# Column sums of a symmetric softmax for two more groups: sixteen accumulating transfers replaced by GpSimd additions

## The chip, the cores and the metric

The kernel runs on one core of one Trainium2 chip. The metric is the device time of one execution in microseconds (us). TensorE is called PE below, VectorE DVE, ScalarE ACT, GpSimd POOL, and the engine whose queue issues most transfers SP, as in the profile.

## The reference, cut to what matters

Four images of 64 x 64 positions with 64 channels, all float32, pass through four layers. Layer 0 is a self-attention over the 4,096 positions of an image, layer 1 a convolution block with a 3 x 3 depthwise convolution, layer 2 an attention without weights, layer 3 a non-local block. The change lies in layer 2, which reads:

```
xf = x.reshape(B, C, N)                        # C = 64, N = 4096, of the array as it lies
scores = einsum('bci,bcj->bij', xf, xf)        # symmetric
attn = softmax(scores, axis=-1)
out = einsum('bcj,bij->bci', xf, attn) + x
```

Layer 1, which the kernel interleaves with it, contains `y = y1 * y2`, `w = mean(y) @ sca_w + sca_b`, `y = y * w`, `y @ pw2_w`: the mean over all positions must be there before the product with `pw2_w`.

## The kernel before, in words

**Layer 2.** The 4,096 rows and columns of the score matrix are split into 8 groups of 512. An item `n` of `layer2` makes one block of 128 x 1024 exponentials: four products on PE (`score`, L1391, with `X` in the tile `ko`), then two exponentials on ACT (L1396), each followed by the read of its row-sum accumulator. The scores are symmetric, so a block of group h can also serve as the mirrored block of group g. For such a mirrored block DVE transposes the exponentials in 32 x 32 pieces (`turned`, L1409), PE multiplies them later (`turned_products`, L1479), and its row sums in the mirror are the column sums of the block: `column_sums` (L1413 to L1434) adds all mirrored blocks of a group into a tile `esum`, folds it once (L1434, 128 x 512) and `spread_sums` (L1442, L1443, DVE) reduces it, nine items after the group's last mirrored block in image 0. Not mirrored blocks are multiplied by `products` (L1453), two or three items behind their score. At a group's end the accumulated products are copied by ACT (L1462 and L1465, tile `own`) and added by DVE into the result `A` (L1468).

**Image 0 and the others.** Images 1 to 3 have a fixed list of groups (`FULL`); POOL adds the column sums there (L1432). Image 0 has the list `PART`: groups 0, 1, 2, 3, 4, 7, 6, 5 in this order, of which groups 0, 1, 6 and 5 have mirrored blocks: 8, 4, 8 and 8. For group 0, POOL adds. For groups 1, 6 and 5 (`moved`), POOL only issues transfers: the first two write the two halves of `esum`, each later one is an accumulating transfer into one half, and a last one adds the halves (L1426, L1430). Two transfers into the same half must follow one another, so POOL waits for the landing of the last but one before it issues the next.

**What sets the order.** The instruction order of PE, ACT, DVE and POOL is written out by hand. Image 0's layer 2 has lanes beside it, generators that advance by estimated times: in the stretch of groups 6 and 5 the lane `conv` runs layer 1 of image 3, and the lane `misc` runs `features2` of image 1 (L1303 to L1314, tile `ko`). In this stretch DVE has, in its order: the last taps of image 3's depthwise convolution (L1241), two multiplications with accumulated sums (L1252: `yg<-y,yg`), their reduction to `ytot` (L1258), the addition of group 7's `own` into `A` (L1468), the four transposes of group 6's first mirrored blocks, then `ch` (L1263, from PE's product L1261 of `ytot`) and `pw2s` (L1265). PE's product L1270 needs `pw2s`.

**Buffers.** Exponentials live in pairs of blocks in tiles of 128 x 2048 from a pool `ep` of six (`new_e`), which `own`, `esum` and image 0's weights tile `xr` (L1361) share. A block's tile is free when its products, its transpose and its column-sum operation (transfer or addition) have read it. In the built program, the ACT block of item 78 (the first not mirrored block after group 6's first four mirrored ones) takes over the tile that was group 7's `own`, and so waits for the DVE addition L1468.

## Time and profile before

| | us |
|---|---|
| median of three runs (2452.43 to 2452.67) | 2452.49 |
| the profiled execution: its time | 2456.51 |
| the profiled execution: its span, first to last instruction | 2454.7 |
| busy PE, of the span | 2417.0 (98%) |
| busy DVE / ACT / POOL | 1479.3 / 1644.3 / 540.9 |
| POOL additions L1432, 128 x 1024: 154 | 2.37 each |
| column-sum transfers L1426: 20, of 512 KB (and 3 by L1430) | 5.5 from issue to landing (median, L1426) |

The profile is one execution, 4.0 us longer than the median of the timed runs and with 1.8 us outside its span. The stretch of the change is the last part of image 0's layer 2: group 6's mirrored blocks stand at 1175 to 1205 us of the span, group 5's at 1214 to 1254.

How to read the lines shown later. A line of the timeline has the start in the span, the time, engine, source line, operation, output<-inputs, shapes, a count, and in brackets the idle time before it with what ended it. Starts overlap with the end of the instruction before[...]. A line of the windows has the stretch, its length, and busy time (and count) of PE, of PE's weight loads, DVE, ACT and POOL, then PE's clock, the busy share of the DMA engines and GB/s. POOL's busy time doesn't count the issue of transfers.

### The profile page before, as it was taken

Reading aid. Unit: us, or ns where it says so; the run is one execution under the profiler, and the core shown is the slowest. Engines: PE = TensorE matmul, PEld = TensorE weight load, DVE = VectorE, ACT = ScalarE, POOL = GpSimd, SP = SyncE. Lnnn points to the kernel's source line nnn. Section 1 sums busy time; section 2 is a strip of 40 time slices with the busy share of each in tenths; the row PEclk is TensorE's granted clock in tenths of the full one; section 3 lists DMA queues with packets and bytes.
Section 4 is the critical chain, followed back from the end, with each engine's and each line's share of the span. In section 5 each row is a group of like instructions: output and inputs, shape, how many; then the busy total and the mean of one; then the engine's idle time right before and its main releaser. Section 6 shows DMA issues by size and latency. Waiting matters only on the chain.

```text
span 2454.7 us, 63654 instructions
## 1 busy us (share of the span) xinstructions
PE 2417.0 (98%) x27509; PEld 916.3 (37%) x27509; DVE 1479.3 (60%) x1794; ACT 1644.3 (67%) x3140; POOL 540.9 (22%) x381
## 2 busy tenths in 40 slices
PE   9999999999999999999999999999999999999998
PEld 3343453336333633343334442144431344421113
DVE  2020278227832773378656668876668866678886
ACT  4656766676666676668654459954479744579996
POOL 2000000000000000120135561255631365622110
PEclk9999999999999999999999999999999999999999
DMA  3000000000000000120630027610075300286554
GB/s 80 1 18 1 19 1 18 18 19 1 18 18 16 4 19 18 35 63 2 136 72 20 19 67 134 139 27 23 16 150 119 78 20 20 71 168 142 120 118 117
DMA packets 66373, 131.68 MB, mean 54 GB/s; under 512 B 12860, under 2 KB 34085, under 8 KB 66085
## 3 DMA queue, kind: packets, MB, share of 16 engines
q0 software_dynamic: 23024, 81.83, 16.5%
q1 hardware_dynamic: 42309, 43.85, 7.9%
q8 instruction: 218, 3.57, 0.6%
q10 hardware_dynamic: 752, 1.85, 0.2%
q14 instruction: 70, 0.57, 0.1%
HBM read 4.80 MB, written 4.19 MB: 4 GB/s over the span
## 4 chain that ended last, share of the span: by engine, by line
PE 86%; DVE 8%; ACT 4%; issue 1%; SPq 0%; DMA 0%; DVEq 0%; ACTq 0%
PE PS L1096 18%; PE PS L1122 18%; PE PS L1391 10%; PE PS L1453 10%; PE PS L1646 8%; PE PS L1707 8%; PE PS L1479 7%; DVE tg L1698 3%; PE PS L1206 2%; ACT e L1657 2%; ACT e L1396 1%; DVE X L1568 1%; PE PS L1561 1%; PE PS L1064 1%; PE PS L1171 1%
## 5 line engine op out<-in xcount | busy, mean ns | idle before, releaser
L1101 ACT ACTIVATE e<-PS 128x1024 f32<-128x1024 f32 x512 | 524.2, 1024 | 339.4 <-PE PS L1096 306.3
L1396 ACT ACTIVATE e<-PS 128x512 f32<-128x512 f32 x632 | 371.6, 596 | 342.0 <-PE PS L1391 321.1
L1096 PE MATMUL PS<-X,q 64*64 64x512 f32 x4096 | 573.9, 591 | 2.3 <-DVE X L979 1.7
L1122 PE MATMUL PS<-e,vq 64*64 64x512 f32 x4096 | 575.3, 592 | 0.0
L1657 ACT ACTIVATE e<-PS 128x512 f32<-128x512 f32 (+2 forms) x588 | 500.2, 921 | 59.0 <-PE PS L1646 38.1
L1698 DVE TENSOR_TENSOR tg<-tg,e 128x2048 f32<-128x2048 f32 x172 | 393.8, 2290 | 42.8 <-ACT e L1657 30.9
L1391 PE MATMUL PS<-ko 64*64 64x512 f32 x2528 | 335.6, 596 | 2.6 <-DVE u L1291 1.5
L1453 PE MATMUL PS<-e,X 64*64 64x512 f32 x2528 | 329.9, 590 | 2.5 <-issue 1.4
L1432 POOL TENSOR_TENSOR esum<-esum,e 128x1024 f32<-128x1024 f32 x132 | 314.0, 2379 | 59.7 <-ACT e L1396 52.4
L1241 DVE SCALAR_TENSOR_TENSOR y<-pad,vec,y 128x1024 f32<-128x1024 f32 x240 | 308.8, 1287 | 18.2 <-ACT y L1237 10.9
L1432 POOL TENSOR_TENSOR esum<-e 128x1024 f32<-128x1024 f32 x22 | 52.2, 2373 | 1206.2 <-ACT e L1396 1187.3
L1409 DVE STREAM_TRANSPOSE turned<-e 128x1024 f32<-128x1024 f32 x196 | 240.6, 1238 | 106.0 <-ACT e L1396 105.8
L1646 PE MATMUL PS<-tg,ph 32*64 32x512 f32 x4096 | 295.1, 612 | 1.7 <-ACT e L1657 0.8
L1096 PEld LDWEIGHTS PS<-X,q 64*64 64x64 f32 x4096 | 183.0, 133 | 261.8 <-issue 181.6
L1122 PEld LDWEIGHTS PS<-e,vq 64*64 64x64 f32 x4096 | 183.1, 133 | 253.8 <-issue 158.1
L1707 PE MATMUL PS<-e,tg 128*32 128x512 f32 x2048 | 272.5, 604 | 0.0
L1109 DVE TENSOR_REDUCE sums<-zs 128x1 f32<-128x4 f32 x128 | 19.6, 153 | 276.4 <-ACT e L1101 276.2
L1679 POOL DMA_DIRECT2D xn<-e x116 | 101.0, 892 | 292.3 <-ACT e L1657 206.0
L1453 PEld LDWEIGHTS PS<-e,X 64*64 64x64 f32 x2528 | 98.0, 133 | 176.3 <-issue 156.7
L1391 PEld LDWEIGHTS PS<-ko 64*64 64x64 f32 x2528 | 90.5, 132 | 169.9 <-issue 145.7
L1646 PEld LDWEIGHTS PS<-tg,ph 32*64 32x64 f32 x4096 | 63.4, 129 | 222.9 <-ACT e L1657 190.5
L1396 ACT ACTIVATION_READ_ACCUMULATOR e<-PS 128x1 f32 x632 | 127.3, 201 | 0.0
(219 smaller groups left out, 1692.4 us busy)
## 6 DMA issues: line engine op xcount, KB each, us to landing
xn<-e POOLq DMA_DIRECT2D x132, 512.0 KB, 5.4
esum<-e POOLq DMA_DIRECT2D x20, 512.0 KB, 5.5
xn<-t SPq DMA_DIRECT2D x64, 128.0 KB
ph<-tg SPq DMA_DIRECT2D x64, 128.0 KB
xn<-X SPq DMA_DIRECT2D x224, 32.0 KB
xr<-X SPq DMA_DIRECT2D x176, 32.0 KB
ko<-ko SPq DMA_DIRECT2D x32, 128.0 KB
xr<-in_x_dram SPq DMA_DIRECT2D x13, 256.0 KB
```

The source lines that it names most:

```text
L1096: mm(ps[64 * c : 64 * c + 64, bass.ts(r, 512)], m.q[rows_, 128 * t + 64 * c : 128 * t + 64 * c + 64], x[rows_, bass.ts(g, 512)], start=Tru ...
L1101: act(es[g // 2][:, bass.ts(g % 2, 1024)], ps, AF.Exp, bias=SHIFT0, accum_out=zs[:, g : g + 1],)
L1122: ins = mm(PS[64 * s : 64 * s + 64, 2048 + 512 * j : 2560 + 512 * j], vq[rows_, :], es[j // 2][rows_, k : k + 512], start=t == 0 and i < 2 ...
L1241: stt(y1, win, wt, y1, ALU.mult, ALU.add)
L1391: mm(ps[64 * c : 64 * c + 64, bass.ts(r, 512)], m.ko[rows_, k : k + 64], m.ko[rows_, bass.ts(h, 512)], start=True, stop=True,)
L1396: act(e[:, bass.ts(r, 512)], ps[:, bass.ts(r, 512)], AF.Exp, bias=SHIFT2, accum_out=slot(g, 2 * u + r),)
L1432: nc.gpsimd.tensor_add(esum, st["e"][mine_t[h][0]] if k == 1 else esum, e)
L1453: mm(st["acc"][r][64 * c : 64 * c + 64, :], xw[rows_, 4 * g + 2 * u + c, :], st["e"][n][rows_, bass.ts(c, 512)], start=n == mine[h][0], st ...
L1646: mm(PS[64 * c : 64 * c + 64, bass.ts(banks[k], 512)], m.ph[32 * k : 32 * k + 32, 128 * mc + 64 * c : 128 * mc + 64 * c + 64], m.th[32 * k ...
L1657: act(e[:, 512 * lo : 512 * k], PS[:, 512 * banks[lo] : 512 * banks[lo] + 512 * (k - lo)], AF.Exp,)
L1698: nc.vector.tensor_add(esum, esum, e)
L1707: mm(st["y"][32 * k : 32 * k + 32, :], m.gx[:, i % 32, :], es[i][:, bass.ts(k, 512)], start=mc == 0, stop=i % 32 == 31,)
```

## The change

In image 0, only group 1 keeps its transfers. Groups 6 and 5 are treated as group 0 and the other images are:

```
             k, e = mine_t[h].index(n), st["e"][n]
-            moved = b == 0 and h > 0
+            moved = b == 0 and h == 1
             if k == (0 if moved else 1):
                 st["esum"][h] = new_e("esum")
```

For each of the two groups, eight transfers L1426 and one L1430 go, and seven additions L1432 (128 x 1024) come. The fold L1434 stays. The tile `esum` is now taken at the second mirrored block instead of the first; no other tile of the pool is taken between the two. In the built program the instruction orders of PE, ACT and DVE are the same as before, and in POOL's order only these rows differ. What ACT and DVE wait for changes with it: where the reuse of a tile waited for a transfer's landing, it now waits for POOL's addition. POOL's first addition of group 6 waits for the second mirrored block's exponentials and for a DVE instruction that is long done.

More of the change, by code (lines that the diff above doesn't have):

```diff
@@ L1417, in column_sums @@
             k, e = mine_t[h].index(n), st["e"][n]
-            moved = b == 0 and h > 0
+            moved = b == 0 and h == 1
             if k == (0 if moved else 1):
```

## The prediction

> **What bounds the kernel now.** I read the page first: PE is busy 98% of the span, and the chain that ended last runs 86% through PE. So time is won or lost only where PE stands still, and each such place counts in full. The windows then say where that is, in the stretch of the change.

> ```profile
> PE 2417.0 (98%) x27509; PEld 916.3 (37%) x27509; DVE 1479.3 (60%) x1794; ACT 1644.3 (67%) x3140; POOL 540.9 (22%) x381
> ...
> PE 86%; DVE 8%; ACT 4%; issue 1%; SPq 0%; DMA 0%; DVEq 0%; ACTq 0%
> ```

> ```profile
> 1176.00:1204.00 28.00, 28.00 (x329) 9.95 (x321) 16.81 (x25) 17.54 (x52) 6.38 (x8) 1.00 0.83 180
> 1215.00:1241.00 26.00, 22.20 (x277) 9.24 (x278) 17.37 (x21) 13.53 (x40) 5.54 (x7) 1.00 0.92 200
> 1241.00:1260.00 19.00, 17.54 (x243) 6.93 (x239) 5.07 (x7) 10.76 (x31) 3.00 (x3) 1.00 0.47 90
> ```

> While group 6 is summed (first row) PE never idles: there is nothing to win there, and something to lose. While group 5 is summed it idles 3.8 us, and 1.5 us behind it. PE's waits in that time name five gaps: 0.83, 0.95 and 0.66 us behind `ko` copies (ACT waits for DVE's copy; no column sum is in that chain), and these two from its timeline:

> ```profile
> 1239.85 0.64 PE L1453 MATMUL PS<-e,X 64*64 64x512 f32 x2 [1.37 <-issue]
> ...
> 1257.51 1.08 PE L1391 MATMUL PS<-ko 64*64 64x512 f32 x6 [1.46 <-DVE u L1291]
> ```

> The first waits for nothing that the program names. It is the only such gap over 0.4 us in the kernel. The packets of PE's instruction queue (16 KB each) explain it: up to it PE began 515 instructions since the last fetch (1215.2, next 1237.4 us). The next longest such runs, 437 and 424, are in the same transfer-laden stretch, all others are at most 383. Fetches are late behind the transfers (DMA engines 92% busy). The second gap is DVE's lateness; its timeline beside POOL's shows why:

> ```profile
> 1253.77 1.76 DVE L1468 TENSOR_TENSOR A<-own,A 128x512 f32<-128x512 f32 x1 [4.21 <-ACT own L1465]
> ...
> 1253.72 1.26 POOL L1434 TENSOR_TENSOR esum<-esum 128x512 f32<-128x512 f32 x1 [3.76 <-DMA esum<-esum]
> ```

> L1468 takes 0.69 us alone (median of 14); here it ends 0.55 us after POOL's fold, 1.07 late.

> **The rule behind this.** [...] the 196 transposes L1409 take 1187 to 1247 ns, though most lie beside POOL additions, while L1298 (two SBUF inputs) takes 691 ns alone and up to 2435 beside one. [...]

> ```profile
> 1609.24 0.69 DVE L1736 SCALAR_TENSOR_TENSOR inv<-inv 128x512 f32<-128x512 f32 x1
> 1609.85 0.08 DVE L1736 DVE_READ_ACCUMULATOR inv<-inv 128x1 f32 x1
> 1609.97 2.73 DVE L1737 SCALAR_TENSOR_TENSOR yz<-inv,yz 128x512 f32<-128x512 f32 x1
> ...
> 1609.71 2.44 POOL L1432 TENSOR_TENSOR esum<-e 128x1024 f32<-128x1024 f32 x1 [26.84 <-ACT e L1396]
> ...
> 1612.22 2.71 POOL L1432 TENSOR_TENSOR esum<-esum,e 128x1024 f32<-128x1024 f32 x1
> ```

> POOL arrives during L1736, gets in 0.55 us after that one's start (2.44 instead of 2.36), DVE's next is held until POOL's end plus 0.55, and POOL's next addition is held 0.35. They alternate. The forecast goes by these durations.

> **The change part by part.**

> *POOL's work.* It loses 18 issues of about 0.86 us and their waits, and gains 14 x 2.37 = 33.2 us of additions. POOL isn't the bound: group 6's blocks come from 1176 to 1199 us, seven additions are 16.6 us, and no SP or ACT queue is passed. Tiles of exponentials come free earlier (addition ends instead of landings 5.5 us after issue); nothing on ACT's path waited for a landing, so this is worth 0.

> *Group 6: the new lock.* Here is DVE's order where the first addition now falls:

> ```profile
> 1177.19 0.69 DVE L1252 SCALAR_TENSOR_TENSOR yg<-y,yg 128x512 f32<-128x512 f32 x1
> 1177.81 0.08 DVE L1252 DVE_READ_ACCUMULATOR yg<-y,yg 128x1 f32 x1
> 1177.81 0.69 DVE L1252 SCALAR_TENSOR_TENSOR yg<-y,yg 128x512 f32<-128x512 f32 x1
> 1178.42 0.08 DVE L1252 DVE_READ_ACCUMULATOR yg<-y,yg 128x1 f32 x1
> 1178.54 0.16 DVE L1258 TENSOR_REDUCE ytot<-ysum 128x1 f32<-128x8 f32 x1
> 1178.62 0.68 DVE L1468 TENSOR_TENSOR A<-own,A 128x512 f32<-128x512 f32 x1
> ```

> ACT's last accumulator read for the second block starts at 1177.14; other additions start at the earliest 0.28 us after such a read's start, so POOL arrives at 1177.42, during the first L1252, and gets in at 1177.74. By the episode's steps:
> - addition 1: 1177.74 to 1180.10. The second L1252 ends at 1180.65 instead of 1178.50.
> - addition 2 (block ready at 1179.2): 1180.52 to 1182.88. L1258 needs no lock (1180.85, still ahead of PE's L1261 at 1181.30); L1468 ends at 1183.43 instead of 1179.30.
> - addition 3: 1183.30 to 1185.66. DVE's four transposes (4.54 us, no lock) run from 1183.36 and L1263 starts at 1187.90, L1265 (`pw2s`) at 1188.11.
> - ACT's item 78 waits for L1468: 1183.5 instead of 1181.42. Items 79 and 80 queue behind it; item 80's last read moves from 1186.39 to about 1186.95, so addition 4 is at 1187.2 to 1189.6. PE's L1391 for item 80 is held about 0.5 us by this, inside the stall below.
> - `pw2s` has one SBUF input, but 64, 128 and 256 columns of such an operation take 254, 287 and 341 ns: 0.45 ns a column against 1.3 for the whole 512-column L1468. [...] it is held: until 1189.7. No row shows one beside POOL; unheld it ends at 1188.4.

> PE's L1270, queued behind nothing at 1185.20, then starts at 1189.75: PE stands 4.55 us (3.2 if `pw2s` isn't held). All of PE, and ACT behind it, moves by this. Later collisions in group 6 (three of the four L1277, about 1.2 us each) end before their readers (ACT's L1165 had 1 to 3 us in hand): 0. **+4.55.**

> *Group 5: the relief.* The transfers' load goes (nine of 512 KB, 4.7 MB, between 1215 and 1254; SP's `xn` and `ko` transfers, 16 of 128 KB, stay), so the fetch is in time: **-1.37**. The fold L1434 follows the last addition at about 1241 instead of 1253.72, so L1468 at 1253.77 meets no lock and PE's 1.46 gap shrinks: **-1.07**. Now L1192 (twice, 1238.4, two SBUF inputs) meets the last addition and the fold: it ends at about 1243.1 instead of 1240.8, and PE needs it at 1247.6 at the earliest: 0. Other DVE work there is transposes and copies from PSUM; L1494's copies from PSUM show the same 414 ns beside POOL as alone: 0. The `ko` gaps stay.

> *Sum.* 4.55 - 1.37 - 1.07 = +2.1 us: the profiled 2456.5 would be 2458.6, and the median, 4.0 below its profile, **2454.6**. Against no change, this kernel's measurement tells about 0.2%, 4.9 us.

> **The rivals.**
> - *POOL comes second (ends faster).* If the two L1252, issued back to back with no wait, keep the pair, addition 1 starts at 1178.36, only L1468 is held (to 1181.27), `pw2s` ends at 1186.2 ahead of addition 4, and PE stands 1.05 us: -1.4, **2451.1**. It decides at 1177.81, 0.4 us after POOL's reckoned arrival. For it: these two have no semaphore between them, the episode's pair had. Against it: 0.07 us lie between the release (0.55 after start) and the second's start.
> - *`pw2s` isn't held:* 3.2 - 2.44 = +0.8, **2453.3**.
> - *The fetch stays late (ends slower).* The lock's stall comes, but SP's own `ko` transfers (1224 to 1240 us) are enough to hold PE's fetch back, so the 1.37 stays: 4.55 - 1.07 = +3.5, **2456.0**. It decides where a fetch run passes some 500 instructions. For it: the gap lies in the `ko` transfers' time. Against it: all three runs over 383 lie where the column sums' transfers do, two of them without `ko` transfers.
> - *The change doesn't do what it says:* excluded, POOL's rows are replaced in the built order and no other order moves.

> **How the numbers follow.** Forecast 0.50 (2454.6, own range 2453.5 to 2455.7), `pw2s` not held 0.12, POOL second 0.15, fetch stays late 0.15, something unlisted 0.08. The range leaves out little more than the last: from POOL second, 2451.1, less 0.3 for the steps' rounding, to 2457.4: the fetch and L1468's 1.07 both not won back (2457.0) and 0.4 for a longer hold. Slower by over 0.2% would need even more than that (2457.4): some of the last two cases, 0.11. Faster by over 0.2% would need all gaps of both groups gone and no stall: 0.02. Within: 0.87.

> **What would show it.** Right: L1252's second and L1468 near 2.8 and 2.7 us at 1178 to 1184; PE L1270 with 4 to 5 us idle before it, released by DVE `pw2s`; no gap without a named wait near 1242, and fetch runs under 400; the last L1468 pair, near 1256 us, back at 0.69 each. Wrong: L1270 without a gap; or a new wait of ACT for POOL behind a tile; or idle PE in group 5 as before.

## The result, and the profile after

| | median, us | runs | lowest to highest |
|---|---|---|---|
| before | 2452.49 | 11 | 2451.61 to 2453.84 |
| after | 2458.60 | 11 | 2457.47 to 2460.41 |

The ratio is 1.0025, 95% interval 1.0016 to 1.0034: the change costs 6.1 us, against a forecast of 2.1 us over the median. The profiled execution of after took 2458.60 us (span 2456.8) and stands at its own median. That of before (2456.51) stood 4.0 above, which turns out to matter. (The title's sixteen transfers are the L1426. Twelve of them accumulate, the first two of each group only write; two accumulating L1430 went with them.)

From the page of after, the busy line and the shares of the chain: PE is still busy 98% of the span, DVE's part of the chain has grown from 8% to 10%.

```profile
PE 2417.7 (98%) x27509; PEld 915.7 (37%) x27509; DVE 1489.3 (61%) x1794; ACT 1642.8 (67%) x3140; POOL 562.5 (23%) x377
...
PE 84%; DVE 10%; ACT 4%; issue 1%; SPq 1%; DMA 0%; DVEq 0%; ACTq 0%
```

The windows of after (stretch, length, PE, PEld, DVE, ACT, POOL, PE's clock, DMA share, GB/s):

```profile
1176.00:1204.00 28.00, 24.11 (x270) 7.95 (x262) 21.43 (x23) 12.29 (x37) 14.95 (x6) 0.94 0.16 39
1215.00:1241.00 26.00, 23.59 (x328) 10.40 (x316) 15.41 (x21) 14.15 (x39) 14.15 (x6) 1.00 0.40 81
1241.00:1260.00 19.00, 18.60 (x268) 7.64 (x260) 10.59 (x13) 11.24 (x33) 4.50 (x2) 1.00 0.01 3
```

In group 6 (first row) PE, which never idled, now idles 3.9 us, and its clock is 0.94 instead of 1.00. In group 5 the two gaps of the first profile of before are gone (PE 23.59 for 22.20, and 18.60 for 17.54). The timelines of DVE and of POOL in group 6:

```profile
1177.08 0.08 DVE L1252 DVE_READ_ACCUMULATOR yg<-y,yg 128x1 f32 x1
1177.08 2.84 DVE L1252 SCALAR_TENSOR_TENSOR yg<-y,yg 128x512 f32<-128x512 f32 x1
...
1180.03 2.64 DVE L1468 TENSOR_TENSOR A<-own,A 128x512 f32<-128x512 f32 x1
1182.60 4.61 DVE L1409 STREAM_TRANSPOSE turned<-e 128x1024 f32<-128x1024 f32 x4
1187.14 0.17 DVE L1263 TENSOR_SCALAR ch<-PS,vec 128x1 f32<-128x1 f32 x1
1187.34 1.66 DVE L1265 TENSOR_SCALAR pw2s<-pw,ch 128x64 f32<-128x64 f32 x1
```

```profile
1176.72 2.64 POOL L1432 TENSOR_TENSOR esum<-e 128x1024 f32<-128x1024 f32 x1 [83.05 <-ACT e L1396]
1179.44 5.46 POOL L1432 TENSOR_TENSOR esum<-esum,e 128x1024 f32<-128x1024 f32 x2
1186.62 2.34 POOL L1432 TENSOR_TENSOR esum<-esum,e 128x1024 f32<-128x1024 f32 x1 [1.71 <-ACT e L1396]
```

POOL's first addition slips in behind the first L1252, the second L1252 and L1468 are each held by one addition (2.84 and 2.64 us for 0.69), the transposes run at their usual rate beside POOL (four in 4.61 us, 4.62 before), and `pw2s` lies inside POOL's fourth addition: 1.66 us for 0.25. “The lock” stands here for just this holding of one engine's operation by the other's; in the prediction, the one that runs meanwhile has “the pair”. PE's timeline shows who waits for `pw2s`:

```profile
1183.51 1.66 PE L1391 MATMUL PS<-ko 64*64 64x512 f32 x8
1189.06 1.72 PE L1270 MATMUL PS<-yg,pw2s 128*64 128x512 f32 x4 [3.89 <-DVE pw2s L1265]
1190.71 1.99 PE L1453 MATMUL PS<-e,X 64*64 64x512 f32 x8
```

PE is idle 3.89 us, and 0.6 more is lost inside the row before (L1391 takes 1.66 for 1.04: item 80's second half waits). But look at the durations *behind* the gap: L1270 x4 takes 1.72 us and L1453 x8 takes 1.99, where the kernel before had no gap and these times:

```profile
1185.20 1.08 PE L1270 MATMUL PS<-yg,pw2s 128*64 128x512 f32 x4
1186.21 1.09 PE L1453 MATMUL PS<-e,X 64*64 64x512 f32 x8
```

The windows of two microseconds of after say why:

```profile
1186.00:1188.00 2.00, 0.00 (x0) 0.00 (x0) 1.97 (x4) 0.47 (x2) 1.39 (x1) 1.00 0.23 57
1188.00:1190.00 2.00, 0.94 (x4) 0.20 (x4) 2.00 (x2) 0.00 (x0) 0.95 (x1) 0.84 0.21 54
1190.00:1192.00 2.00, 2.00 (x10) 0.30 (x8) 0.52 (x2) 0.78 (x1) 0.00 (x0) 0.50 0.20 50
1192.00:1194.00 2.00, 2.00 (x52) 1.13 (x56) 0.33 (x1) 0.00 (x0) 0.00 (x0) 0.81 0.20 49
1194.00:1196.00 2.00, 2.00 (x88) 1.61 (x73) 0.00 (x0) 0.00 (x0) 0.00 (x0) 1.00 0.17 41
```

**Bookkeeping.** I compare the starts of the same PE instructions in two traces. Against a later, undisturbed profile of before (e1, 2452.46 us), after is 0.17 us late at the start of the stretch, 4.76 late at L1270 and 6.37 at 1225 us, where it stays. So the stall is 4.59, and the slow clock 1.61. Their sum, 6.2, is the whole measured difference of 6.1.

### The profile page after: what moved, and what is told of

Same layout as the page of the kernel before. It is cut to its first block, busy times and chain, and to the rows that moved or that the text cites. A ratio compares the mean times of both kernels' runs of the same rounds, so it can differ in the third digit from the quotient of the medians.

```text
span 2456.8 us, 63634 instructions
## 1 busy us (share of the span) xinstructions
PE 2417.7 (98%) x27509; PEld 915.7 (37%) x27509; DVE 1489.3 (61%) x1794; ACT 1642.8 (67%) x3140; POOL 562.5 (23%) x377
## 4 chain that ended last, share of the span: by engine, by line
PE 84%; DVE 10%; ACT 4%; issue 1%; SPq 1%; DMA 0%; DVEq 0%; ACTq 0%
PE PS L1096 18%; PE PS L1122 18%; PE PS L1453 8%; PE PS L1391 8%; PE PS L1646 8%; PE PS L1707 8%; PE PS L1479 7%; DVE tg L1698 3%; PE PS L1206 2%; ACT e L1657 2%; DVE y L1241 2%; DVE turned L1409 1%; ACT e L1396 1%; PE PS L1270 1%; DVE X L1568 1%
## 5 line engine op out<-in xcount | busy, mean ns | idle before, releaser
L1396 ACT ACTIVATE e<-PS 128x512 f32<-128x512 f32 x632 | 370.8, 595 | 341.0 <-PE PS L1391 318.6
L1432 POOL TENSOR_TENSOR esum<-esum,e 128x1024 f32<-128x1024 f32 x144 | 343.0, 2382 | 78.1 <-ACT e L1396 70.4
L1432 POOL TENSOR_TENSOR esum<-e 128x1024 f32<-128x1024 f32 x24 | 57.2, 2382 | 1312.8 <-ACT e L1396 1304.6
L1391 PE MATMUL PS<-ko 64*64 64x512 f32 x2528 | 334.6, 596 | 1.6 <-ACT ko L1313 0.8
L1453 PE MATMUL PS<-e,X 64*64 64x512 f32 x2528 | 328.3, 592 | 1.1 <-ACT own L1465 1.1
L1409 DVE STREAM_TRANSPOSE turned<-e 128x1024 f32<-128x1024 f32 x196 | 240.6, 1237 | 101.3 <-ACT e L1396 101.2
L1453 PEld LDWEIGHTS PS<-e,X 64*64 64x64 f32 x2528 | 97.4, 133 | 174.4 <-issue 154.7
L1391 PEld LDWEIGHTS PS<-ko 64*64 64x64 f32 x2528 | 90.1, 132 | 169.7 <-issue 145.4
L1396 ACT ACTIVATION_READ_ACCUMULATOR e<-PS 128x1 f32 x632 | 127.2, 201 | 0.0
```

The lines of the kernel that those rows point to most:

```text
L1391: mm(ps[64 * c : 64 * c + 64, bass.ts(r, 512)], m.ko[rows_, k : k + 64], m.ko[rows_, bass.ts(h, 512)], start=True, stop=True,)
L1396: act(e[:, bass.ts(r, 512)], ps[:, bass.ts(r, 512)], AF.Exp, bias=SHIFT2, accum_out=slot(g, 2 * u + r),)
L1432: nc.gpsimd.tensor_add(esum, st["e"][mine_t[h][0]] if k == 1 else esum, e)
L1453: mm(st["acc"][r][64 * c : 64 * c + 64, :], xw[rows_, 4 * g + 2 * u + c, :], st["e"][n][rows_, bass.ts(c, 512)], start=n == mine[h][0], st ...
```

## The experiments

**Was the first profile of before a usual one? (e1)** The kernel before, once more.

> The kernel before, unchanged, profiled once more. Theory A (the relief in group 5 exists only in the one profiled execution of before, which was 4.0 us longer than its timed runs): this profile has a different pattern of gaps, its span nearer to 2450.7 (2452.5 less 1.8) and the nameless 1.37 us gap of PE near 1240 us absent or smaller. Theory B (the gaps are in every execution, and the changed kernel loses 3.5 us elsewhere): the same gaps of 1.37 and 1.46 us again.

It took 2452.46 us (27 timed runs of before on that chip: median 2453.05). Its windows, and PE's row behind `u`:

```profile
1215.00:1241.00 26.00, 23.57 (x303) 9.68 (x295) 16.47 (x20) 14.66 (x44) 5.12 (x7) 1.00 0.97 207
1241.00:1260.00 19.00, 18.61 (x264) 7.66 (x264) 6.51 (x10) 12.25 (x32) 3.02 (x3) 1.00 0.41 79
```

```profile
1253.11 1.09 PE L1391 MATMUL PS<-ko 64*64 64x512 f32 x8 [0.39 <-DVE u L1291]
```

With the transfers in place and the DMA engines busier than in the first profile (0.97), there is no nameless gap, and the gap behind `u` is 0.39 us, not 1.46. PE is as busy as in after. What I had booked as relief was not there to be won in this execution.

**Each group alone (e2, e3).** One word of the change: in e2 only group 6 goes to POOL, in e3 only group 5.

```
-            moved = b == 0 and h == 1
+            moved = b == 0 and h in (1, 5)      # e2
+            moved = b == 0 and h in (1, 6)      # e3
```

> Only group 6 goes to POOL; groups 1 and 5 keep their transfers. Theory A: the whole loss is here, PE's 4.55 us stall before L1270 and 1.5 us of half clock behind it, so +6.1 (2458.6). Theory B: without group 5's relief the loss is larger, +9.5 (2462).

> Only group 5 goes to POOL; groups 1 and 6 keep their transfers. Theory A: nothing to win back in timed runs, 0 within 0.6 us (2452.5). Theory B: the relief of 1.9 + 0.4 + 1.1 us seen in the profiles is real, -3.5 (2449.0).

e2: 2459.47 us, ratio 1.0027 (1.0016 to 1.0039), PE's gap ahead of L1270 3.90 us, its clock again 0.50 behind it. e3: 2453.30, ratio 1.0001 (0.9992 to 1.0009), no gap but the three `ko` ones and 0.40 behind `u`, as in e1. The whole loss comes from group 6; group 5 is worth nothing that can be measured, and a gain of the 2.4 us forecast lies outside its interval.

**The lock without the collision (e4).** As after, but POOL begins group 6 one mirrored block later, when the L1252 pair and L1468 are done:

```
-            if k == (0 if moved else 1):
+            begin_at = 0 if moved else 2 if b == 0 and h == 6 else 1
+            if k == begin_at:
...
-                nc.gpsimd.tensor_add(esum, st["e"][mine_t[h][0]] if k == 1 else esum, e)
+                nc.gpsimd.tensor_add(esum, st["e"][mine_t[h][0]] if k == begin_at else esum, e)
+                if k == begin_at == 2:
+                    nc.gpsimd.tensor_add(esum, esum, st["e"][mine_t[h][1]])
```

> Both groups on POOL, but group 6's additions begin at the third mirrored block (third plus first, then the second, then as before), about 2 us later, when DVE's L1252 pair and L1468 are done. If the lock on those three makes the stall: no gap before L1270, no half clock, and the time of before less the relief: Theory A 2452.5, Theory B 2449. If something else of POOL's additions makes it: still +6, 2458.6.

It took 2452.66 us, ratio 0.9999 (0.9990 to 1.0007), with the same seven additions. Its DVE (L1471 is L1468 there) and PE:

```profile
1176.97 0.69 DVE L1252 SCALAR_TENSOR_TENSOR yg<-y,yg 128x512 f32<-128x512 f32 x1
...
1177.78 0.68 DVE L1471 TENSOR_TENSOR A<-own,A 128x512 f32<-128x512 f32 x1
...
1183.13 0.28 DVE L1265 TENSOR_SCALAR pw2s<-pw,ch 128x64 f32<-128x64 f32 x1
```

```profile
1184.35 1.08 PE L1270 MATMUL PS<-yg,pw2s 128*64 128x512 f32 x4
```

Nothing is held, PE has no gap, and all 6.1 us are back. It isn't POOL's additions as such that cost time, but where the first of them falls. It doesn't beat the kernel before either: there was no gain to keep.

**Is `pw2s` held by POOL? (e5)** As after, but addition 4 of group 6 (`k == 4`, the group's fifth mirrored block) is issued one block later, behind addition 5:

```
+                if b == 0 and h == 6 and k == 4:
+                    return
                 nc.gpsimd.tensor_add(esum, st["e"][mine_t[h][0]] if k == 1 else esum, e)
+                if b == 0 and h == 6 and k == 5:
+                    nc.gpsimd.tensor_add(esum, esum, st["e"][mine_t[h][4]])
```

> The changed kernel, but POOL adds group 6's fourth mirrored block one block later (then two additions in a row), so no addition runs when DVE has pw2s. Theory A (pw2s is held by addition 4 under the lock[...]): L1265 takes about 0.25 us instead of 1.66, PE's gap before L1270 is about 2.5 us instead of 3.9, no half clock follows, and the kernel is +3.2 us on the kernel before (about 2456). Rival B (pw2s is late for another reason): the gap stays at 3.9 and the cost at +6. Rival C (an idle of 2.5 us halves the clock too): the gap is 2.5 us and the cost +4.7.

```profile
1187.42 0.25 DVE L1265 TENSOR_SCALAR pw2s<-pw,ch 128x64 f32<-128x64 f32 x1
```

```profile
1187.73 0.65 PE L1270 MATMUL PS<-yg,pw2s 128*64 128x512 f32 x2 [2.48 <-DVE pw2s L1265]
```

Without an addition beside it `pw2s` takes 0.25 us, PE's gap is 2.48, and the clock stays 1.00. PE loses 3.18 us in the trace; the median is 2456.31 against 2452.88 for before (+3.4), ratio 1.0015 (1.0008 to 1.0021). B falls, and C for this execution, which is the fastest of the 21 timed ones, 0.9 us under their median. Between the traces of after and e5 this hold costs 1.4 us by itself, and 1.6 more because the clock fell in one and not in the other.

**Idle time alone (e6, e7, e9).** Is the slow clock the price of the idle, whatever makes it? The kernel before, with N idle transposes ahead of `pw2s` (N = 4, 6 and 8; each took 0.75 us rather than my 0.6, so the idle came out longer than expected), no lock and no addition moved:

```
+        if b == B - 1:
+            dead = y1.rearrange("p w h -> p (w h)")
+            for i in range(N):
+                nc.vector.transpose(dead[:, 0:512], x[:, 0:512])
         pw2s = sm.tile([128, C], F32, tag="pw2s", name="pw2s", bufs=1)
```

> The kernel before, with four idle transposes (128 x 512, about 0.6 us each, into a dead tile) ahead of pw2s in image 3's layer 1: PE stands before L1270, with no lock of POOL. PE had 0.95 us in hand, so the idle is about 1.45 us. Theory A [...]: +1.45 us, PE clock stays 1.00. Rival C (the clock halves after any idle over 1 us): +3.0 us.

> As the last, with six transposes: idle about 2.65 us. Theory A: +2.65 us, clock 1.00. Rival C: +4.2 us.

> As the last, with eight transposes: idle about 3.85 us. Theory A (the half clock in the changed kernel comes from the length of the idle, whatever made it): PE's clock is about 0.5 for some 3 us behind it and the cost is about +5.4 us. Rival D (the half clock comes with the lock or the transfers of the changed kernel, not with idle time): +3.85 us, clock 1.00.

PE's rows of N = 6, then of N = 8 (four lines were added, so L1274 is L1270 there):

```profile
1188.14 1.08 PE L1274 MATMUL PS<-yg,pw2s 128*64 128x512 f32 x4 [3.21 <-DVE pw2s L1269]
```

```profile
1189.82 1.98 PE L1274 MATMUL PS<-yg,pw2s 128*64 128x512 f32 x4 [4.71 <-DVE pw2s L1269]
```

The same four products take 1.08 us behind an idle of 3.21 and 1.98 behind one of 4.71. Rival D falls: no lock is needed. C falls for N = 4 and for this execution of N = 6. The median times are 2455.34, 2459.14 and 2461.25 us against 2452.88; ratios 1.0010 (1.0003 to 1.0016), 1.0022 (1.0013 to 1.0031), 1.0032 (1.0019 to 1.0044). These are 0.7, 3.0 and 1.7 us above what the traces show for stall plus slow clock, so in time N = 6 fits neither theory.

The length of the idle isn't the whole of it. Here are stretches that begin and end where the clock changes, or whole multiples of 3.41 us from there: N = 8, then N = 6, then the end of the kernel in e3.

```profile
1183.84:1187.25 3.41, 1.27 (x12) 0.15 (x4) 3.27 (x5) 2.13 (x8) 0.54 (x1) 1.00 1.04 201
1187.25:1190.66 3.41, 0.84 (x2) 0.30 (x4) 3.31 (x6) 0.00 (x0) 0.33 (x1) 0.50 1.00 190
1190.66:1194.07 3.41, 3.41 (x20) 0.63 (x24) 0.95 (x2) 0.78 (x1) 0.00 (x0) 0.50 0.33 81
1194.07:1197.49 3.42, 3.42 (x132) 2.48 (x116) 0.00 (x0) 0.00 (x0) 0.00 (x0) 1.00 0.18 43
```

```profile
1183.36:1186.77 3.41, 1.58 (x16) 0.31 (x8) 3.27 (x7) 2.44 (x8) 0.23 (x1) 1.00 1.05 198
1186.77:1190.19 3.42, 2.05 (x15) 0.42 (x15) 2.54 (x5) 0.78 (x1) 0.63 (x1) 1.00 0.88 172
```

```profile
2438.97:2442.38 3.41, 1.53 (x13) 1.08 (x11) 1.08 (x2) 1.92 (x3) 0.00 (x0) 1.00 0.97 296
2442.38:2445.79 3.41, 0.00 (x0) 0.00 (x0) 0.00 (x0) 0.00 (x0) 0.00 (x0) 0.50 1.02 402
```

In N = 8 the clock falls at 1187.25, only 2.1 us into the idle. In each of the 13 traces the clock's changes lie whole multiples of 3.41 us apart (in before 713 times 3.413; in after 345, 346 and 714 times, counted from the first). Where the clock was full, it fell at the end of every such stretch in which PE stood idle for 1.88 us or more (e3 has the least), and of none with 1.83 or less (N = 6 has the most). An idle of 2.48 or 3.21 us can lie across two stretches so that neither holds that much. That is how it lay in the traces of e5 and N = 6, which was luck, since the stretches lie elsewhere in another execution. Laid over their places in the 13 traces, the idle of N = 6 would slow the clock in 9 or 10 and that of e5 in 6 or 7 (an estimate from these traces).

**Does the late fetch exist?** The trace of N = 6 has the nameless gap again, in group 5 (L1457 is L1453 there), with the gap behind `u` also back at 1.47:

```profile
1242.02 0.64 PE L1457 MATMUL PS<-e,X 64*64 64x512 f32 x2 [0.62 <-issue]
```

So it isn't a fault of one profile. I took N = 4 with group 5 summed by POOL (e10: N = 4 and e3's word), N = 4 again beside it (e11), and a third profile of before (e12).

> The kernel before with the four idle transposes ahead of pw2s, and with group 5 (not group 6) summed by POOL. Theory F (group 5's transfers do delay PE's fetch, but only in some executions, more often when PE comes 1 to 3 us later to that place; a run of 500 or more instructions since the last fetch leaves PE without code): the times lie close together at about +1.8 us on the kernel before (the idle's length, 2454.6), none above 2457, and below the same kernel with group 5's transfers by about 0.8 us in the median. Rival G (group 5's transfers cost nothing in any execution but the one profile): same median and same spread as the kernel with transfers.

> The four idle transposes alone, again, on the same chip as the last: theory F: median about 2455.3 with a third of the executions above 2455.5. Rival G: as the last kernel.

> The kernel before, a third profile. Theory F: the nameless gap of PE near 1240 us appears only if PE began 500 or more instructions since its last fetch there; with a shorter run there is none, and L1391 behind u waits 0.4 us. Rival G: no gap whatever the run is.

e10 gave 2455.04 us (ratio 1.0007, 0.9999 to 1.0015), e11 2455.49 (1.0011, 1.0003 to 1.0020), before 2452.54. The difference of 0.45 has the sign of F and half its size, but the intervals cover each other and three of e10's 13 times are above F's 2457, up to 2459.3: inconclusive in the times. The traces are clearer. Here are all those with group 5's transfers, by the largest number of instructions that PE began between two fetches at 1215 to 1245 us, with what PE lost against e1 between 1236 and 1245:

| trace | instructions between fetches | nameless gap, us | PE lost, us |
|---|---|---|---|
| before, first profile | 515 | 1.37 | 2.4 |
| N = 6 | 508 | 0.62 | 1.7 |
| N = 8 | 500 | 0.13 | 1.2 |
| N = 4, second | 500 | 0.15 | 1.2 |
| N = 4, first | 476 | none | 0 |
| e2 | 420 | none | 0 |
| before, e1 and e12 | 374, 372 | none | 0 |

Without these transfers the number is 324 at most (after, e3, e4, e5, e10), and nothing is lost. So the nameless gap goes with the number, and the point of decision lies at some 500, as the prediction had it. That PE waits for its instructions there is argued from this order; no trace names the wait. Before shows the gap in one profile of three, and "fetches are late behind the transfers" isn't enough: what makes a fetch come early or late, at the same load of the DMA engines, stays open.

**An unasked answer.** e12 took 2458.77 us. Its group 5 was undisturbed; this time another place had failed, 1000 us later, where ACT waited 4.83 us for a transfer into `xn`:

```profile
2209.84 1.98 PE L1646 MATMUL PS<-tg,ph 32*64 32x512 f32 x6 [3.51 <-ACT e L1657]
```

```profile
2208.00:2210.00 2.00, 0.16 (x3) 0.16 (x6) 0.89 (x1) 0.81 (x2) 0.00 (x0) 0.93 0.73 165
2210.00:2212.00 2.00, 2.00 (x10) 0.34 (x14) 1.90 (x2) 1.74 (x3) 0.00 (x0) 0.50 0.40 92
2212.00:2214.00 2.00, 2.00 (x16) 0.33 (x16) 1.90 (x2) 1.33 (x1) 0.00 (x0) 0.50 0.00 0
2214.00:2216.00 2.00, 2.00 (x20) 0.20 (x8) 2.00 (x1) 0.35 (x1) 0.00 (x0) 0.50 0.00 0
2216.00:2218.00 2.00, 2.00 (x24) 0.23 (x16) 1.90 (x2) 1.59 (x2) 0.00 (x0) 0.86 0.00 0
```

An idle of 3.51 us, on another engine's account, is followed by half clock in the unchanged kernel as well, and here that cost 3.1 us, nearly as much as the stall (3.3).

## Why the prediction was wrong, point by point

The miss is 4.0 us over the median (2458.6 for 2454.6), and two steps of the sum make it up. The stall was costed at its own length, with nothing for the slow clock behind it (1.6 us), and a relief was subtracted that the usual execution didn't have to give (2.4 us).

- **The lock's arrival and order: right.** The traces' starts differ by 0.73 us ahead of group 6. With that added, the second L1252 ends at 1180.65 (reckoned 1180.65), L1468 at 1183.40 (1183.43), L1263 starts at 1187.87 (1187.90), `pw2s` ends at 1189.73 (1189.7) and L1270 starts at 1189.79 (1189.75). L1258 wasn't held, as reckoned: 0.16 us inside addition 2, as without one. "POOL comes second" is refuted. The one episode at 1609 us was enough to compute these steps. The later collisions came too (three L1277 at 1.74 to 1.86 us, L1192 twice at 4.60 for 2.32 together) and moved PE by less than 0.1 us, as reckoned.
- **`pw2s` is held: right,** though no trace of before showed it: it was the author's estimate, argued from the rate per column. It took 1.66 us beside POOL and 0.25 without (e5). The stall of 3.2 us, reckoned for a `pw2s` that isn't held, is just what e5 lost (3.18), with the hold removed.
- **"PE stands 4.55 us. All of PE, and ACT behind it, moves by this": the stall right, the sum mis-sized.** The stall is 4.59 (3.89 of it idle, not the 4 to 5 listed under what would show it, since 0.6 went in the row before); PE's movement is 6.2. The missing term is the half clock behind it, 1.6 us. The step costed an idle at its own length. The trace of before had no idle as long as the stall in this stretch (1.46 us is its longest there), so it couldn't warn me. Of the idles shown below, the three up to 3.21 us didn't slow the clock and the four from 3.51 did. But their length isn't what decided, since the clock of N = 8 fell 2.1 us into the idle; what parts the rows is the fourth column, the most idle time in one of the 3.41 us stretches (for N = 8, in the one that ended with the fall):

| kernel, what held PE | idle shown, us | PE late by, us | most idle in one stretch, us | then lost to the clock, us | lowest clock |
|---|---|---|---|---|---|
| N = 4, filler | 1.72 | 1.79 | 0.98 | 0 | 1.00 |
| e5, lock | 2.48 | 3.18 | 1.57 | 0 | 1.00 |
| N = 6, filler | 3.21 | 3.27 | 1.83 | 0 | 1.00 |
| N = 8, filler | 4.71 | 4.77 | 2.14 | 1.95 | 0.50 |
| after, lock | 3.89 | 4.59 | 3.11 | 1.6 | 0.50 |
| e12, a transfer | 3.51 | 3.29 | 3.38 | 3.1 | 0.50 |
| e2, lock | 3.90 | 4.60 | 3.41 | 1.6 | 0.50 |

- **The relief of group 5, -2.44: failed.** What the gap goes with was read rightly (the table of fetches), and after does lack both gaps. But they were the accident of one execution, not a cost of the kernel: e1 and e12 have neither, and e3 measures what group 5's part does to the time as +0.2 us (-2.0 to +2.2 by its interval). The second gap came from the first: the fold waits for transfers and keeps its time (1253.30 in e1, 1253.72 in the first profile), while L1468, carried along by PE, came at 1250.44 in e1, well ahead of the fold, and at 1253.77 in the late profile, just behind its start. Behind the short gaps of N = 8 and the second N = 4 the gap behind `u` stays at 0.39. In e1 DVE had both additions done before POOL began:

```profile
1250.44 1.42 DVE L1468 TENSOR_TENSOR A<-own,A 128x512 f32<-128x512 f32 x2 [4.21 <-ACT own L1465]
```

```profile
1253.30 1.27 POOL L1434 TENSOR_TENSOR esum<-esum 128x512 f32<-128x512 f32 x1 [3.75 <-DMA esum<-esum]
```

- **"The median, 4.0 below its profile": failed with it.** Those 4.0 us held 3.5 us of just these two gaps (2.4 for the fetch, with what follows its gap, and 1.07). I subtracted their relief from the profile and then the same excess again to come to the median: counted twice. The profiled executions do differ by the forecast 2.1 (2458.60 against 2456.51), but by the sum 4.59 + 1.61 - 3.50 - 0.7 of the start-up, not by mine: that agreement is luck.
- **"The fetch stays late" (2456.0):** refuted in its place; the fetches of after are at most 316 instructions apart there, so `ko`'s transfers alone don't delay them.
- **Range and chances.** The range (2450.8 to 2457.4) doesn't hold 2458.6. Its upper end let the whole relief fail (2457.0) but gave only 0.4 us to a stall that costs more; with the slow clock's 1.6 in that place it is the measured 2458.6. Slower by over 0.2%, held for 0.11 likely, came (0.25%).

Not settled: N = 4 to 8 measured 0.7 to 3.0 us above what their traces show of stall and clock. The late fetch (1.2 and 1.7 us in the profiles of N = 8 and N = 6) and, for N = 6, a clock that falls in many executions would fill most of that: 5 of its 11 timed runs have a mean clock of 0.997, which none of the 48 of before beside them has. No trace of such an execution was taken. For e5 the medians leave only 0.2 us for a clock that falls in some executions. e10, without transfers in group 5, is also 0.7 above its stall of 1.78, inside its interval.

## What to carry to other kernels

Price a stall of PE by two numbers: its length, and another 1.6 to 3.1 us for the half clock if the clock falls. By these traces that takes about 1.9 us of idle in one 3.41 us stretch, and where the stretches lie isn't known beforehand. So, as an estimate from the 1.83 and 1.88 us above, a stall under 1.9 us is safe, one over twice that always pays, and one between pays in some executions. Shortening a stall from 3.9 to 2.5 us paid 3.0 in the traces and 2.7 in the medians. Before a gap of one profile is booked as winnable, look whether the execution stands at the median: an execution 4 us above it shows gaps that the others don't have, and a gain taken from them must not be taken again as the distance to the median. When work moves to POOL, place its first operations behind DVE operations with two SBUF inputs that PE waits for (L1252 and L1468 took 2.84 and 2.64 us in after, 0.69 and 0.68 in e4); one block later was enough here.

## What the runs showed of the hardware

- The price of a half clock doesn't follow the idle's length: 3.51 us of idle cost 3.1 behind it, 4.71 cost 1.95, since in the latter a part of the slow time (2.57 us) passed while PE was idle. The slow time is 3.4 us in after and 6.8 in e12 and in N = 8, once and twice the same length. It ended with the first 3.41 us stretch that PE all but filled: 3.33 us of PE did it in e2, 3.29 did not in e12.
- A DVE operation of 64 columns with one SBUF input and a scalar was held 1.4 us by a POOL addition (1.66 for 0.25), while four transposes L1409 took 4.61 us beside additions and 4.62 without.
- PE's loss at a late fetch exceeded the nameless gap by about 1.1 us in all four traces that have it (2.4 for 1.37, 1.7 for 0.62, 1.2 for 0.13 and for 0.15).
